# Which attention steps carry the routing arithmetic, and when a new head pair's first values are issued

## The chip, the cores and the metric

The kernel runs on one core of a Trainium2 chip. TensorE (PE in the profile) multiplies matrices, and its weight loads are listed apart as PEld. VectorE is DVE, ScalarE is ACT, GpSimd is POOL, and SyncE (SP) issues transfers. The metric is the device time of one execution in microseconds; the median of several runs counts.

## The reference

The input is 8 items of 256 channels by 32x32 positions, so S=1024 tokens of 256 numbers. Each item goes through a layer of attention over its tokens, a second layer of attention with a norm, and a mixture of experts. Layer 0, which the change concerns, has 8 heads of 64 and takes its softmax over the queries (`axis=1`):

```python
xt = x.reshape(B, C, S).transpose(0, 2, 1)
qkv = (xt @ w_qkv + b_qkv).reshape(B, S, N_HEADS, 3 * D_K)
q, k, v = jnp.split(qkv, 3, axis=-1)
attn = jnp.einsum('bihd,bjhd->bijh', q, k) * SCALE
attn = jax.nn.softmax(attn, axis=1)
res = jnp.einsum('bijh,bjhd->bihd', attn, v).reshape(B, S, N_HEADS * D_K)
res = res @ w_out + b_out + xt
```

The mixture sends every token to the best two of 8 experts:

```python
probs = jax.nn.softmax(logits, axis=-1)
rw, re = jax.lax.top_k(probs, TOP_K)
```

The two weights are divided by their sum, and each chosen expert (matrix, gelu, matrix) adds its weighted result to the token.

## The kernel before

All arithmetic is float32. The loop over items runs layer 0 of item b (`layer0`), then its second attention and norm. The routing of item b is a Python generator, `dispatch`, which is handed to `layer0` of item b+1 and advanced from within it. Experts for items 0 to 6 come after the last layer 0; item 7 is done densely. So layer 0 of item 0 carries no routing, that of items 1 to 7 does.

**Layer 0.** The 8 heads are handled as 4 pairs g, and each pair has 8 blocks j of 128 keys. That is 32 steps, `steps[at]`, and a tail of `LAG` = 2. A score tile has 128 keys on the partitions and 1024 queries. For each step and head h:

- `score(at, h, n)` multiplies keys and queries for one half n of the queries into a two-bank PSUM tile (`psc`). Every matmul uses a 64x64 quarter of the array; four of them, called a set here, run at once in the four quarters. A set is eight records in the profile.
- `first_max` (L410) and `soften` find the maximum of the two halves on VectorE (L410 and L422). ScalarE then takes the exponential and its sum (L432).
- `divide` puts the softmax's divisor into the values (L441, L443).
- `gather_values(at, turn)`, two steps later, multiplies exponentials and values into two one-bank tiles, `po[0]` and `po[1]` (L463). In turn 0 the upper key half goes to one tile and the lower to the other; in turn 1 they change places. Before a row half of the array writes a tile that the other half has just written, a relay (L473) must have seen that one end: a nop on GpSimd for item 0, on SP for the others.

So TensorE's queue for a step is: scores of (at, head 0, half 0) with those of (at−1, head 1, half 1); values of at−2, turn 0; scores of (at, head 0, half 1) with those of (at, head 1, half 0); values of at−2, turn 1.

**PSUM.** Three two-bank buffers (`big`) serve score tiles, projections (`pqk`), the routing's counts (`pcn`) and transposes in turn. Two one-bank buffers (`acc`) hold `po`. When a pair's last values are gathered, ScalarE copies both `po` to `res` (L482); the next pair's first values are written to the same two buffers.

**Projections.** Queries and keys of the next pair are made by `project` in steps j=3 and j=5 of the first three pairs, hence steps 3, 5, 11, 13, 19 and 21. Each has four full-array matmuls (L300, eight records) and two evictions on VectorE (L290).

**Routing.** `gates` makes a softmax over 8 logits for each token and finds the best and second best (about twenty VectorE operations on 128x64, L656 to L725). `dispatch` counts, with two small matmuls into `pcn` (L743, L744), how many tokens before each one go to the same expert. It works out a target row for each token, casts it to an integer (L795) and writes the token there with an indirect transfer on GpSimd (L797): 16 scatters for an item, each with its cast. Before the change the generator is advanced once in step 0 and once in each step from 2 on. Its slice is issued after the step's values of turn 1 and after `first_max(at, 1)`, so it stands on VectorE between the two maxima of (at, head 1). In steps with a projection it is issued after the projection.

A tile framework orders each engine's instructions as they are issued, except where `tc.issue_after` holds one back, and finds the semaphore waits. `tc.add_manual_dep(..., BEHIND)` adds a wait.

Of the kernel before, what the change touches and what calls it, by code (L numbers as in the profile page):

```python
# [11 lines left out]
I32 = mybir.dt.int32  # L12
# [7 lines left out]
def kernel(  # L20
# [349 lines left out]
    def layer0(b, xT, begun, routing):  # L370
# [8 lines left out]
        res = one.tile([P, NPAIR, S], F32, tag="res", name=f"res_{b}")  # L379
        steps = [(g, j) for g in range(NPAIR) for j in range(NT)]  # L380
        LAG = 2
        seconds, turned = {}, {}

        relay = nc.gpsimd if b == 0 else nc.sync
# [98 lines left out]
            return mm  # L483

        last = len(steps) - 1
        for at in range(last + LAG + 1):
            if at <= last:
                score(at, 0, 0)
            if 0 < at <= last + 1:
                score(at - 1, 1, 1)  # L490
                soften(at - 1, 1)
            if at >= LAG:
                gather_values(at - LAG, 0)
            if at <= last:

                with tc.issue_after(seconds[1].ins) if 1 in seconds else nullcontext():
                    first_max(at, 0)
                score(at, 0, 1)
                score(at, 1, 0)
                soften(at, 0)  # L500
                with tc.issue_after(seconds[0].ins):
                    ahead = divide(at - 1) if at > 0 else seconds[0]
                with tc.issue_after(ahead.ins):
                    first_max(at, 1)
            elif at == last + 1:
                divide(last)
            if at == 0:
                begun.rest()
                next(routing, None)
            if at >= LAG:  # L510
                array = gather_values(at - LAG, 1)
            if at <= last:
                g, j = steps[at]
                if g + 1 < NPAIR and j in (3, 5):
                    if j == 3:
                        qks.append([])
                    qks[g + 1].append(project(b, xT, g + 1, len(qks[g + 1])))
                if array is not None:
                    with tc.issue_after(firsts[at, 1].ins), tc.issue_after(array.ins):
                        next(routing, None)  # L520
        for _ in routing:
            pass

# [117 lines left out]
    def gates(b, lT):  # L641


        def tmp(tag):
            return small.tile([P, NT, E], F32, tag=tag, name=f"{tag}_{b}", bufs=1)

        def col(tag):
            return small.tile([P, NT], F32, tag=tag, name=f"{tag}_{b}", bufs=1)

        n = S // NG  # L650
        pt = acc(f"plT_{b}")
        for j in range(n // P):
            nc.tensor.transpose(pt[:, ts(j, P)], lT[:, ts(j, P)], ident)

        l = tmp("g_l")
        nc.vector.tensor_copy(  # L656
            l.rearrange("p (g j) e -> p j g e", g=NG),
            pt[:, :n].rearrange("p (j g e) -> p j g e", g=NG, e=GC)[:, :, :, :E],
        )
        yield  # L660
        m = col("g_m")
        nc.vector.tensor_reduce(m, l, AX.X, ALU.max)
        p = tmp("g_p")
        nc.vector.tensor_sub(p, l, bcast(m, E))
        nc.scalar.activation(p, p, AF.Exp)
        yield
        z = col("g_z")
        nc.vector.tensor_reduce(z, p, AX.X, ALU.add)
        nc.vector.reciprocal(z, z)
        nc.vector.tensor_mul(p, p, bcast(z, E))  # L670
        yield

        def first_of_max(src, tag):
            top, best = col(f"{tag}_top"), col(f"{tag}_best")
            hot = tmp(f"{tag}_hot")
            nc.vector.tensor_reduce(top, src, AX.X, ALU.max)
            nc.vector.tensor_tensor(hot, src, bcast(top, E), ALU.is_equal)
            yield
            nc.vector.tensor_mul(hot, hot, rank)
            nc.vector.tensor_reduce(best, hot, AX.X, ALU.max)  # L680
            nc.vector.tensor_tensor(hot, hot, bcast(best, E), ALU.is_equal)
            return top, hot

        top1, hot1 = yield from first_of_max(p, "g_1")
        yield
        rest = tmp("g_rest")
        nc.vector.scalar_tensor_tensor(rest, hot1, -2.0, p, ALU.mult, ALU.add)
        top2, hot2 = yield from first_of_max(rest, "g_2")
        yield
        total = col("g_total")  # L690
        nc.vector.tensor_add(total, top1, top2)
        nc.vector.tensor_scalar_max(total, total, 1e-12)
        nc.vector.reciprocal(total, total)
        gate = keep.tile([P, 2, NT], F32, tag="gate", name=f"gate_{b}")
        nc.vector.tensor_mul(gate[:, 0], top1, total)
        nc.vector.tensor_mul(gate[:, 1], top2, total)
        return gate, (hot1, hot2)
# [30 lines left out]
    def dispatch(b, n2, l, group):  # L728

        gate, hots = yield from gates(b, l)  # L730
        yield

        def tmp(tag):
            return small.tile([P, NT, E], F32, tag=tag, name=f"{tag}_{b}", bufs=1)


        both = tmp("d_both")
        nc.vector.tensor_add(both, hots[0], hots[1])
        yield
        yield  # L740
        pcn = big(f"pcn_{b}")
        flat = both.rearrange("p i e -> p (i e)")
        nc.tensor.matmul(pcn[:, : NT * E], before, flat, start=True, stop=True)  # L743
        nc.tensor.matmul(pcn[:, NT * E : 2 * NT * E], ones, flat, start=True, stop=True)  # L744
        cn = small.tile([P, 2, NT, E], F32, tag="d_cn", name=f"d_cn_{b}", bufs=1)
        nc.vector.tensor_copy(cn.rearrange("p t i e -> p (t i e)"), pcn[:, : 2 * NT * E])
        yield
        per = small.tile([P, E, NT], F32, tag="d_per", name=f"d_per_{b}", bufs=1)
        nc.vector.tensor_copy(per, cn[:, 1].rearrange("p i e -> p e i"))
        upto = small.tile([P, E, NT], F32, tag="d_upto", name=f"d_upto_{b}", bufs=1)  # L750
        nc.vector.tensor_tensor_scan(
            upto.rearrange("p e i -> p (e i)"),
            later.rearrange("p e i -> p (e i)"),
            per.rearrange("p e i -> p (e i)"),
            0.0,
            ALU.mult,
            ALU.add,
        )
        yield
        rows = tmp("d_rows")  # L760
        nc.vector.tensor_sub(rows.rearrange("p i e -> p e i"), upto, per)
        nc.vector.tensor_add(rows, rows, cn[:, 0])
        counts = keep.tile([P, E], F32, tag="counts", name=f"counts_{b}")
        if group.counts is None:
            nc.vector.tensor_copy(counts, upto[:, :, NT - 1])
        else:
            nc.vector.tensor_add(
                rows, rows, group.counts.unsqueeze(1).to_broadcast([P, NT, E])
            )
            nc.vector.tensor_add(counts, group.counts, upto[:, :, NT - 1])  # L770
        group.counts = counts

        kept = []
        tos = []
        for k in range(2):
            yield
            hot = hots[k]
            sel = tmp("d_sel")
            nc.vector.tensor_mul(sel, hot, rows)
            row = keep.tile([P, NT], F32, tag=f"row{k}", name=f"row{k}_{b}")  # L780
            nc.vector.tensor_reduce(row, sel, AX.X, ALU.add)
            nc.vector.tensor_mul(sel, hot, e_iota.unsqueeze(1).to_broadcast([P, NT, E]))
            exp = keep.tile([P, NT], F32, tag=f"exp{k}", name=f"exp{k}_{b}")
            nc.vector.tensor_reduce(exp, sel, AX.X, ALU.add)
            yield
            to = small.tile([P, NT], F32, tag="d_to", name=f"d_to_{b}_{k}", bufs=2)
            nc.vector.scalar_tensor_tensor(to, exp, float(group.cap), row, ALU.mult, ALU.add)
            kept.append((row, exp))
            tos.append(to)
            group.kept[b] = gate, kept  # L790

        for k in range(2):
            for i in range(NT):
                at = small.tile([P, 1], I32, tag="d_at", name=f"d_at_{b}_{i}_{k}", bufs=4)
                nc.vector.tensor_copy(at, tos[k][:, i : i + 1])  # L795
                view = group.views[2 * (NT * group.items.index(b) + i) + k]
                nc.gpsimd.indirect_dma_start(  # L797
                    out=view[:, :],
                    out_offset=bass.IndirectOffsetOnAxis(ap=at, axis=0),
                    in_=n2[:, i, :],  # L800
                    in_offset=None,
                )
                yield

    def plan(group):

# [371 lines left out]
    begun = Begin(0, next_x)  # L1178
    begun.all()
    prepare()  # L1180
    routing = iter(())
    for b in range(B):
        xT = next_x
        if b + 1 < B:
# [65 lines left out]
```

## Time and profile before

| what | us |
| --- | --- |
| median of 3 runs | 2530.41 (2528.81 to 2532.02) |
| the profiled execution | 2521.92 |
| its span, first to last instruction | 2520.2 |
| TensorE busy | 2421.3 |
| VectorE busy | 1565.1 |
| ScalarE busy | 887.7 |
| GpSimd busy | 386.4 |
| layer-0 scores, L395 on TensorE | 613.4 |
| layer-0 values, L463 on TensorE | 612.8 |

A line of a group names the source line, engine and operation, output and inputs, count, busy time and mean duration in ns, and then the engine's idle time just before these instructions with what ended most of it. A line of the table of waits gives the engine and line that waited, for whom, the total in us, the number of times and the longest. A line of the timeline gives start, duration, engine, line and count, and in brackets the idle time before it with what ended it. TensorE counts as busy while any quarter of it works.

### The profile page before, as it was taken

Reading aid. Unit: us, or ns where it says so; the run is one execution under the profiler, and the core shown is the slowest. Engines: PE = TensorE matmul, PEld = TensorE weight load, DVE = VectorE, ACT = ScalarE, POOL = GpSimd, SP = SyncE. Lnnn points to the kernel's source line nnn. Section 1 sums busy time; section 2 is a strip of 40 time slices with the busy share of each in tenths; the row PEclk is TensorE's granted clock in tenths of the full one; section 3 lists DMA queues with packets and bytes.
Section 4 is the critical chain, followed back from the end, with each engine's and each line's share of the span. In section 5 each row is a group of like instructions: output and inputs, shape, how many; then the busy total and the mean of one; then the engine's idle time right before and its main releaser. Section 6 shows DMA issues by size and latency. Waiting matters only on the chain.

```text
span 2520.2 us, 37152 instructions
## 1 busy us (share of the span) xinstructions
PE 2421.3 (96%) x14015; PEld 1334.8 (53%) x14015; DVE 1565.1 (62%) x3836; ACT 887.7 (35%) x1491; POOL 386.4 (15%) x383
## 2 busy tenths in 40 slices
PE   9999999999999999999999999999999999997799
PEld 3356434653465346533663356335633688875466
DVE  5774677468755884578557855875578643334443
ACT  2541355125512561246225521552154422211222
POOL 0000002000200020002000100010001344434452
PEclk9999999999999999999999999999999999998899
DMA  7992001000100000000000000000001266653353
GB/s 281 385 361 69 34 3 44 6 17 1 35 17 17 1 30 21 17 1 28 24 17 1 25 27 17 1 22 14 1 18 49 91 214 213 217 186 101 98 162 119
DMA packets 82556, 188.23 MB, mean 75 GB/s; under 512 B 13992, under 2 KB 23880, under 8 KB 80584
## 3 DMA queue, kind: packets, MB, share of 16 engines
q1 hardware_dynamic: 57368, 118.65, 13.1%
q0 software_dynamic: 25008, 67.20, 8.6%
q8 instruction: 111, 1.82, 0.3%
q14 instruction: 69, 0.57, 0.1%
HBM read 100.49 MB, written 110.90 MB: 84 GB/s over the span
## 4 chain that ended last, share of the span: by engine, by line
PE 72%; DVE 9%; ACT 3%; issue 2%; DMA 1%; another core or an unknown queue 1%; ACTq 0%; DVEq 0%; SPq 0%; POOLq 0%
PE po L463 13%; PE psc L395 12%; PE pqk L300 8%; PE py L602 7%; PE ps L576 6%; PE pr L542 4%; PE ph L937 4%; PE pe L962 3%; PE pv L336 3%; DVE scrap L422 3%; PE pdy L1144 2%; PE pdh L1120 2%; PE px L561 2%; PE pa L595 2%; ACT ex L432 2%
## 5 line engine op out<-in xcount | busy, mean ns | idle before, releaser
L432 ACT ACTIVATE ex<-psc,nmax 128x1024 f32<-128x1024 f32 x512 | 571.1, 1115 | 528.2 <-DVE scrap L422 408.9
L463 PE MATMUL po<-ex,vs 64*64 64x512 f32 x4096 | 612.8, 593 | 25.4 <-ACT res L482 21.3
L395 PE MATMUL psc<-qk,qk 64*64 64x512 f32 x4096 | 613.4, 596 | 17.3 <-ACT ex L432 16.3
L422 DVE TENSOR_SCALAR_CACHE_REDUCE scrap<-psc,nmax 128x512 f32<-128x512 f32 x512 | 383.9, 750 | 118.3 <-PE psc L395 98.7
L410 DVE TENSOR_REDUCE nmax<-psc 128x1 f32<-128x512 f32 x512 | 350.5, 684 | 11.9 <-PE psc L395 11.9
L395 PEld LDWEIGHTS psc<-qk,qk 64*64 64x64 f32 x4096 | 188.0, 132 | 320.7 <-issue 167.8
L463 PEld LDWEIGHTS po<-ex,vs 64*64 64x64 f32 x4096 | 187.2, 132 | 285.0 <-issue 91.3
L602 PE MATMUL py<-n,aT 128*128 128x256 f32 x1024 | 243.5, 392 | 19.3 <-DVE aT L597 14.5
L797 POOL DMA_INDIRECT rows<-n,d_at x112 | 109.3, 976 | 926.1 <-DVE d_at L795 919.7
L602 PEld LDWEIGHTS py<-n,aT 128*128 128x128 f32 x1024 | 195.4, 195 | 84.2 <-DVE aT L597 52.3
L576 PE MATMUL ps<-nT,xa 128*128 128x512 f32 x512 | 236.5, 592 | 0.0
L300 PE MATMUL pqk<-xT,wqkv 128*128 128x512 f32 x512 | 235.0, 602 | 0.1
L587 ACT ACTIVATE ex<-ps,nmax 128x1024 f32<-128x1024 f32 x64 | 71.3, 1115 | 353.7 <-DVE nmax L584 338.5
L607 DVE SCALAR_TENSOR_TENSOR t<-py,rs,t 128x256 f32<-128x256 f32 x64 | 31.0, 484 | 234.3 <-PE py L602 202.3
L723 POOL TENSOR_TENSOR t<-t,n 128x2048 f32<-128x2048 f32 x8 | 36.3, 4533 | 901.6 <-issue 631.3
L300 PEld LDWEIGHTS pqk<-xT,wqkv 128*128 128x128 f32 x512 | 93.3, 190 | 133.0 <-issue 92.8
L576 PEld LDWEIGHTS ps<-nT,xa 128*128 128x128 f32 x512 | 93.6, 190 | 79.9 <-issue 73.6
L1009 POOL DMA_INDIRECT yk<-y,yat x112 | 112.6, 1006 | 122.4 <-DVE o L1041 71.5
L290 DVE TENSOR_SCALAR qk<-pqk,b_qk 128x512 f32<-128x512 f32 x100 | 75.1, 751 | 85.1 <-PE pqk L300 85.1
L336 PE MATMUL pv<-wqkv,xT 128*128 128x512 f32 x256 | 119.6, 597 | 0.8 <-ACT wqkv L106 0.8
L584 DVE TENSOR_REDUCE nmax<-ps 128x1 f32<-128x1024 f32 x64 | 78.3, 1223 | 59.1 <-PE ps L576 58.6
L542 PE MATMUL pr<-wo,res 128*128 128x256 f32 x512 | 111.8, 379 | 0.0
(191 smaller groups left out, 2441.4 us busy)
## 6 DMA issues: line engine op xcount, KB each, us to landing
rows<-wb SPq DMA_DIRECT2D x7, 8192.0 KB
y<-yb SPq DMA_DIRECT2D x63, 256.0 KB
xT<-in_x_dram SPq DMA_DIRECT2D x7, 1024.0 KB
sums<-t SPq DMA_DIRECT2D x7, 1024.0 KB
o<-sums SPq DMA_DIRECT2D x7, 1024.0 KB
out_dram<-oT SPq DMA_DIRECT2D x14, 512.0 KB
wpack<-in_L_ffn_w_dram SPq DMA_DIRECT2D x4, 1024.0 KB
wb<-in_L_ffn_w_dram SPq DMA_DIRECT2D x16, 256.0 KB
```

The lines of the kernel that those rows point to most:

```text
L300: mm = nc.tensor.matmul(pq[:, ts(n, 512)], wqkv[:, cc, t, ts(g, P)], xT[:, cc, ts(n, 512)], start=(cc == 0), stop=(cc == NCC - 1),)
L336: nc.tensor.matmul(pv, self.xT[:, cc, ts(i, P)], wqkv[:, cc, 2, :], start=(cc == 0), stop=(cc == NCC - 1),)
L395: mm = nc.tensor.matmul(pss[at, h][ts(c, DK), ts(n, 512)], k[r, j * P + c * DK : j * P + (c + 1) * DK], q[r, ts(n, 512)], start=True, stop ...
L410: firsts[at, h] = nc.vector.tensor_reduce(nmax, pss[at, h][:, ts(0, 512)], AX.X, ALU.max, negate=True)
L422: seconds[h] = nc.vector.tensor_scalar(scrap, ps[:, ts(1, 512)], -1.0, nmaxes.pop((at, h)), ALU.mult, ALU.min, accum_out=nmax,)
L432: nc.scalar.activation(ex, ps, AF.Exp, bias=nmax, scale=1.0, accum_out=sums[at][:, h : h + 1])
L463: mm = nc.tensor.matmul(po[n][ts(h, DK), :], vss[at][keys, h, :], exps[at, h][keys, ts(n, 512)], start=(j == 0 and turn == 0), stop=(j == ...
L542: nc.tensor.matmul(pr[:, :C], res[:, g, ts(i, P)], wo[:, g, :], start=(g == 0), stop=(g == NPAIR - 1))
L576: nc.tensor.matmul(psc[:, ts(n, 512)], xa[:, ec, ts(i, P)], nT[:, ec, ts(n, 512)], start=(ec == 0), stop=(ec == NCC - 1),)
L602: nc.tensor.matmul(py[:, :D], aT[:, ts(m, P)], n1[:, m, :], start=(m == 0), stop=(m == NT - 1))
L797: nc.gpsimd.indirect_dma_start(out=view[:, :], out_offset=bass.IndirectOffsetOnAxis(ap=at, axis=0), in_=n2[:, i, :], in_offset=None,)
L1009: nc.gpsimd.indirect_dma_start(out=yk[:, i, k, :], out_offset=None, in_=self.group.y[:, :], in_offset=bass.IndirectOffsetOnAxis(ap=ats[k][ ...
```

## The change

Routing is advanced in step 0 and in the steps of a projection only: steps 3, 5, 11 and 13 hold all of its arithmetic, and it is now issued before the projection. Most `yield`s go; five slices are left: from the logits to the exponential's argument (step 0), softmax and best expert (3), second best and gates (5), counts and row numbers (11), target rows (13). The sixteen casts of 128x1 become two of 128x8. The scatters come one a step from step 14 to 29, each with an added wait for that step's `first_max(at, 1)`.

In the steps 10, 18 and 26, where a new pair's first values are gathered, turn 0 of these values is issued after the step's second score set, directly ahead of turn 1.

```diff
+        PROJECT = [(0, 3), (0, 5)]
+        PROJECT += [(g, j) for g in range(1, NPAIR - 1) for j in (3, 5)]
+        FIRST_SCATTER = PROJECT[3]
...
+        def share(behind=None):
+            try:
+                routing.send(behind)
+            except StopIteration:
+                pass
+
         for at in range(last + LAG + 1):
+            g, j = steps[min(at, last)]
+            late = at > LAG and steps[at - LAG][1] == 0 and (g, j - 1) not in PROJECT
...
-            if at >= LAG:
+            if at >= LAG and not late:
                 gather_values(at - LAG, 0)
...
             if at == 0:
                 begun.rest()
-                next(routing, None)
+                share()
+            if late:
+                gather_values(at - LAG, 0)
             if at >= LAG:
                 array = gather_values(at - LAG, 1)
-            if at <= last:
-                g, j = steps[at]
-                if g + 1 < NPAIR and j in (3, 5):
-                    if j == 3:
-                        qks.append([])
-                    qks[g + 1].append(project(b, xT, g + 1, len(qks[g + 1])))
-                if array is not None:
-                    with tc.issue_after(firsts[at, 1].ins), tc.issue_after(array.ins):
-                        next(routing, None)
+            project_now = at <= last and (g, j) in PROJECT
+            if at <= last and (project_now or (g, j) > FIRST_SCATTER):
+                with tc.issue_after(firsts[at, 1].ins), tc.issue_after(array.ins):
+                    share(firsts[at, 1])
+            if project_now:
+                if len(qks) == g + 1:
+                    qks.append([])
+                qks[g + 1].append(project(b, xT, g + 1, len(qks[g + 1])))
...
         for k in range(2):
...
+            at = small.tile([P, NT], I32, tag=f"d_at{k}", name=f"d_at{k}_{b}", bufs=1)
+            nc.vector.tensor_copy(at, to)
+            ats.append(at)
+        group.kept[b] = gate, kept
 
         for k in range(2):
             for i in range(NT):
-                at = small.tile([P, 1], I32, tag="d_at", name=f"d_at_{b}_{i}_{k}", bufs=4)
-                nc.vector.tensor_copy(at, tos[k][:, i : i + 1])
+                behind = yield
...
-                nc.gpsimd.indirect_dma_start(
+                scatter = nc.gpsimd.indirect_dma_start(
...
-                    out_offset=bass.IndirectOffsetOnAxis(ap=at, axis=0),
+                    out_offset=bass.IndirectOffsetOnAxis(ap=ats[k][:, i : i + 1], axis=0),
...
-                yield
+                if behind is not None:
+                    tc.add_manual_dep(scatter.ins, behind.ins.name, BEHIND)
```

More of the change, by code (lines that the diff above doesn't have):

```diff
@@ L670, in gates @@
         nc.vector.tensor_mul(p, p, bcast(z, E))
-        yield
         def first_of_max(src, tag):
@@ L677, in first_of_max @@
             nc.vector.tensor_tensor(hot, src, bcast(top, E), ALU.is_equal)
-            yield
             nc.vector.tensor_mul(hot, hot, rank)
@@ L682, in first_of_max @@
             return top, hot
-        top1, hot1 = yield from first_of_max(p, "g_1")
-        yield
+        top1, hot1 = first_of_max(p, "g_1")
         rest = tmp("g_rest")
         nc.vector.scalar_tensor_tensor(rest, hot1, -2.0, p, ALU.mult, ALU.add)
-        top2, hot2 = yield from first_of_max(rest, "g_2")
         yield
+        top2, hot2 = first_of_max(rest, "g_2")
         total = col("g_total")
@@ L730, in dispatch @@
         gate, hots = yield from gates(b, l)
-        yield
         def tmp(tag):
@@ L738, in dispatch @@
         nc.vector.tensor_add(both, hots[0], hots[1])
-        yield
         yield
@@ L746, in dispatch @@
         nc.vector.tensor_copy(cn.rearrange("p t i e -> p (t i e)"), pcn[:, : 2 * NT * E])
-        yield
         per = small.tile([P, E, NT], F32, tag="d_per", name=f"d_per_{b}", bufs=1)
@@ L758, in dispatch @@
         )
-        yield
         rows = tmp("d_rows")
@@ L773, in dispatch @@
         kept = []
-        tos = []
+        ats = []
+        yield
         for k in range(2):
-            yield
             hot = hots[k]
@@ L784, in dispatch @@
             nc.vector.tensor_reduce(exp, sel, AX.X, ALU.add)
-            yield
             to = small.tile([P, NT], F32, tag="d_to", name=f"d_to_{b}_{k}", bufs=2)
@@ L788, in dispatch @@
             kept.append((row, exp))
-            tos.append(to)
-            group.kept[b] = gate, kept
+            at = small.tile([P, NT], I32, tag=f"d_at{k}", name=f"d_at{k}_{b}", bufs=1)
+            nc.vector.tensor_copy(at, to)
+            ats.append(at)
+        group.kept[b] = gate, kept
         for k in range(2):
             for i in range(NT):
-                at = small.tile([P, 1], I32, tag="d_at", name=f"d_at_{b}_{i}_{k}", bufs=4)
-                nc.vector.tensor_copy(at, tos[k][:, i : i + 1])
+                behind = yield
                 view = group.views[2 * (NT * group.items.index(b) + i) + k]
-                nc.gpsimd.indirect_dma_start(
+                scatter = nc.gpsimd.indirect_dma_start(
                     out=view[:, :],
-                    out_offset=bass.IndirectOffsetOnAxis(ap=at, axis=0),
+                    out_offset=bass.IndirectOffsetOnAxis(ap=ats[k][:, i : i + 1], axis=0),
                     in_=n2[:, i, :],
@@ L802, in dispatch @@
                 )
-                yield
+                if behind is not None:
+                    tc.add_manual_dep(scatter.ins, behind.ins.name, BEHIND)
     def plan(group):
@@ L1180 @@
     prepare()
-    routing = iter(())
+    routing = (nothing(_) for _ in ())
     for b in range(B):
```

## The prediction, made before the changed kernel ran

> **What bounds the kernel.** I read the page's head first, then its costliest groups.
>
> ```profile
> span 2520.2 us, 37152 instructions
> PE 2421.3 (96%) x14015; PEld 1334.8 (53%) x14015; DVE 1565.1 (62%) x3836; ACT 887.7 (35%) x1491; POOL 386.4 (15%) x383
> ...
> L463 PE MATMUL po<-ex,vs 64*64 64x512 f32 x4096 | 612.8, 593 | 25.4 <-ACT res L482 21.3
> L395 PE MATMUL psc<-qk,qk 64*64 64x512 f32 x4096 | 613.4, 596 | 17.3 <-ACT ex L432 16.3
> ```
>
> TensorE is busy for 96% of the span; everything else has slack on average. So an edit is worth only the TensorE idle it removes, or time in which only half of the array works. The two layer-0 groups show 43 us of counted idle before them. The table of waits names the releasers:
>
> ```profile
> PE po L463 <- ACT res L482: 21.3, 24, 0.9
> PE psc L395 <- ACT ex L432: 16.3, 39, 2.3
> ```
>
> 24 is 8 items by 3 borders between head pairs, 0.89 us each: the first values of a new pair wait until ScalarE has copied the old pair's sums out of PSUM. That is what the second half of the change addresses. What routing costs must be found by comparison, because half-array gaps are not counted as idle. Item 0 routes nothing. Cutting the trace into one stage per item, from the first step's scores to the last's (columns: busy time and count of PE, PEld, DVE, ACT, POOL; clock; DMA), gives items 2, 3 and 0:
>
> ```profile
> 544.50:684.80 140.30, 135.75 (x1030) 53.78 (x1030) 112.87 (x315) 77.67 (x130) 13.20 (x14) 1.00 0.05 19
> 801.10:941.40 140.30, 135.74 (x1030) 53.75 (x1030) 112.88 (x315) 77.66 (x130) 13.16 (x14) 1.00 0.05 19
> 28.60:165.00 136.40, 133.27 (x1024) 52.17 (x1024) 105.82 (x262) 76.12 (x128) 0.00 (x0) 1.00 1.03 382
> ```
>
> Routing adds 3.9 us to layer 0 of an item. Taking the starts of the first row maximum (L410) of successive steps, I split this: step 0 +0.41, steps 2 to 5 +0.07, 6 to 9 +1.25, 10 to 13 +0.95, 14 to 17 +1.26, later nothing. An undisturbed step takes 3.43 us.
>
> The mechanism, VectorE in item 3, and TensorE's weight load after it:
>
> ```profile
> 834.78 0.21 DVE L687 SCALAR_TENSOR_TENSOR g_rest<-g_hot,g_p 128x64 f32<-128x64 f32 x1
> 835.02 0.22 DVE L676 TENSOR_REDUCE g_top<-g_rest 128x8 f32<-128x64 f32 x1
> 835.28 0.23 DVE L677 TENSOR_TENSOR g_hot<-g_rest,g_top 128x64 f32<-128x64 f32 x1
> 835.42 0.74 DVE L422 TENSOR_SCALAR_CACHE_REDUCE scrap<-psc,nmax 128x512 f32<-128x512 f32 x1
> ...
> 837.52 0.21 PEld L395 LDWEIGHTS psc<-qk,qk 64*64 64x64 f32 x8 [1.05 <-ACT ex L432]
> ```
>
> Three small operations stand between the two maxima of a step, so the second maximum is 0.65 us late, its exponential too, and the next scores wait for that score buffer (1.05 us before the load, about 0.5 in a quiet step).
>
> [...] The trace has 214 to 232, so I use about 0.25 us start to start for dependent routing operations. [...] at a border the waiting G holds back the scores queued behind it, although those need nothing of it. [...] a relay of a nop on another engine stands between the two turns; it stays. [...]
>
> **The routing part.** It takes VectorE work out of the steps without projection and puts it into the steps with one (3, 5, 11, 13) and step 0. Removed: the excess of steps 2–5, 6–9 and 14–17, 0.07+1.25+1.26 = 2.58 us per item; 98 of 112 casts go too (143 ns each).
>
> What is added in a projection step must hide. The projection's eight records occupy TensorE 3.43 us, and VectorE's extra work there is two evictions of 0.75 us. Step (0,3) gets 9 operations (2.2 us), (0,5) 11 (some independent, about 1.6), (1,3) the counts' 6–7, (1,5) 12 (about 2.3). Starting 1.04 us after the projection does, the longest bunch puts the second eviction's end at about 4.77 us and the second maximum at 4.79 us from its own scores: it just hides. I charge 0.05 us per item; without cover, (0,3) and (1,5) would cost up to their full 4.5. At step 0 VectorE idles 0.45 us after the copy of the logits, against 0.49 for the two operations moved in: nothing to 0.04; the 0.41 of that step stays.
>
> Of the 16 scatters, each stays one GpSimd instruction (0.97 us), now one a step from step 14 to 29, behind that step's first maximum. GpSimd is 15% busy, its scatters waited 919.7 us on casts, and in items 1 to 7 the relay is on SP. They end before the experts' gather needs them: I charge zero. Late scatters would cost only if the last item's moved past its 1981.3 fetch.
>
> One thing gets worse. The two count matmuls `pcn` now stand before the projection of step 11. Before, in item 2:
>
> ```profile
> 597.25 3.70 PE L300 MATMUL pqk<-xT,wqkv 128*128 128x512 f32 x8
> 600.79 0.33 PE L743 MATMUL pcn<-d_both,before 128*128 128x64 f32 x2
> 600.96 0.39 PE L744 MATMUL pcn<-d_both,ones 128*128 128x64 f32 x2
> 601.27 1.18 PE L395 MATMUL psc<-qk,qk 64*64 64x512 f32 x5
> ```
>
> There the third score buffer went to pqk, and the next scores waited for pqk's second eviction: 0.93 us over item 0. After, pcn takes the buffer free first and the projection itself must wait for the exponential of step 11, which ends 1.42 us after the step's scores began; 1.16 to 1.40 us. Loss 0.23 to 0.47; I take 0.47.
>
> Sum: 2.58 − 0.47 − 0.05 ≈ 2.05, times 7 items = 14.4 us. Bounds: 10 if the bunches in (0,3) and (1,5) together delay a maximum by 0.6, 18 if pcn costs no more than before.
>
> **The border part.** Border of item 0, TensorE and then ScalarE:
>
> ```profile
> 71.06 1.04 PE L395 MATMUL psc<-qk,qk 64*64 64x512 f32 x8
> 73.01 1.13 PE L463 MATMUL po<-ex,vs 64*64 64x512 f32 x6 [0.91 <-ACT res L482]
> 73.92 0.60 PE L395 MATMUL psc<-qk,qk 64*64 64x512 f32 x2
> ```
> ```profile
> 71.27 1.11 ACT L432 ACTIVATE ex<-psc,nmax 128x1024 f32<-128x1024 f32 x1 [0.34 <-DVE rs L441]
> 72.38 1.06 ACT L482 COPY res<-po 128x512 f32<-128x512 f32 x2
> ```
>
> The exponential must end (72.38) before two copies run; the first gives its buffer at 73.0, the second at 73.49. Row halves then run 0.49 us apart until the next full-array matmul. A border costs 1.46 us over 3.43 in its own step, and 0.15 more at the next projection: 1.61 for two borders of an item, 1.46 for the third.
>
> After, the two score sets come first. S(10,0,1) runs 71.92–72.53; S(10,1,0) needs the buffer of that same exponential, so 72.53–73.39. The values still start at 73.01 in one row half and 73.49 in the other, each half as it comes free. Turn 1 follows at once, without a score set between, and so sees the relay openly. The trace has this case once, at the end of layer 0 of the last item:
>
> ```profile
> 1979.13 2.32 PE L463 MATMUL po<-ex,vs 64*64 64x512 f32 x16 [0.33 <-issue]
> ```
>
> Turn to turn is 1.23 there, not 0.86: 0.37 us for matmul end, nop, restart. So turn 1 starts at about 74.40 and 74.70 and the next step's scores at about 75.6 in both halves (before 75.63 and 76.12). Gain 0.5 where the skew used to be paid at the next projection, about 0.4 at the third border: 8 × (0.5+0.5+0.4) = 11.2. Bounds: 1 (0.04 each, if the halves stay skewed) and 21.3 (the whole counted wait).
>
> Total: −14.4 − 11.2 ≈ −25.6. The profiled execution was 2521.9 us for a span of 2520.2, and would be 2496.3. The median of the runs is 8.5 above the profiled one: 2530.4 − 25.6 ≈ **2505 us**.
>
> **Rivals.**
> *Border gain nil.* The chain exponential, copy, copy, values, relay, values has the same length whatever stands in the wait; if the next scores or their exponential hang on it, only 1 of 11.2 comes: −15.4, 2515. For it: both copies and the relay stay. Against: 1.7 us of score work moves into a wait.
> *Border wait gone.* If the relay is covered by the other row half, −21.3 − 14.4: 2495. For it: halves run independently. Against: 1979.13.
> *Bunches don't hide.* If eviction or maximum is pushed in four steps, the routing gain goes and −11.2 is left: 2519; the whole change breaks even at 25.6/7 = 3.7 us per item, near the 4.5 without cover. For it: only 0.02 us of slack in (1,5).
> *Slower: the open relay.* A nop on SP stands behind SP's fetches and stores. A score set hid its delay; back to back nothing does. Above 0.37 + 0.47 + 14.4/24 ≈ 1.44 us of relay at each of 24 borders the change loses; at 2.0 it gives −14.4 + 24 × (1.63 − 0.47) = +13.4: 2544. For it: TensorE's loads waited 42.9 us on SP, 128 times. Against: the longest was 1.0.
> *No effect.* It cannot be void: the built instruction order differs at exactly 24 borders and 7 pcn places on TensorE.
>
> **Chances and range.** Likeliest 0.46 (own range 2499 to 2511), border gain nil 0.19, wait gone 0.17, bunches 0.11, open relay 0.07. The unknowns' bounds give −11 to −39, 2491 to 2519; I take 2492 to 2520, leaving out the relay's case and the tail of the bunches. 0.2%, 5 us, is about what a measurement of this kernel can tell from no change. Faster 0.90 (a quarter of the bunches' case not), same 0.03, slower 0.07.
>
> **What would show it.** Layer 0 of items 2 to 6 at about 136.9 us (138.2 less 1.4 at borders), item 0 at 135.0; steps 6–9 and 14–17 as in item 0; step 11 about 0.4 longer; the wait of po on res below 10 us or gone, with SP in its place, about 0.4 each; border steps 4.4 instead of 4.89. Wrong if projection steps grow over 7.1, or if border steps keep 4.9.

## The result, and the profile after

| | before, us | after, us |
| --- | --- | --- |
| median of 4 runs each | 2530.69 (2528.81 to 2532.02) | 2503.53 (2499.54 to 2504.45) |
| the profiled execution | 2521.92 | 2504.45 |
| layer 0, sum over the 8 items | 1130.4 | 1103.4 |
| layer 0 of item 0 (no routing) | 136.34 | 134.95 |
| layer 0 of items 2 to 6, mean | 140.31 | 136.88 |
| layer 0 of item 7 | 145.90 | 141.04 |
| from there to the end | 546.5 | 556.3 |

The ratio is 0.989 with a 95% interval of 0.9873 to 0.9907: 27.2 us less between the medians, against 25.6 forecast. "Layer 0" is, here and below, the time from the first step's first row maximum to the last step's, read from the trace. The head of the page after, and the two groups of layer 0:

```profile
span 2502.8 us, 37112 instructions
PE 2420.1 (97%) x14015; PEld 1324.5 (53%) x14015; DVE 1565.8 (63%) x3738; ACT 887.6 (35%) x1491; POOL 389.0 (16%) x383
...
L399 PE MATMUL psc<-qk,qk 64*64 64x512 f32 x4096 | 585.9, 594 | 7.3 <-ACT ex L436 7.2
L467 PE MATMUL po<-ex,vs 64*64 64x512 f32 x4096 | 578.9, 593 | 5.6 <-DVE vs L447 4.1
```

The groups' busy times fell by 28 and 34 us, although the matmuls are the same in number and, to 2 ns, in their mean duration, and TensorE's busy time as a whole is the same. The likely reading is that a group counts as busy while any quarter works for it: where one row half runs behind the other, scores and values run at the same time and both are counted. The counted idle before the two groups fell from 43 to 13 us. What TensorE, its weight loads on the last line, wait for now:

```profile
PE psc L399 <- ACT ex L436: 7.2, 11, 2.6
PE pqk L300 <- ACT ex L436: 4.9, 7, 0.7
PEld po L467 <- SPq L477: 60.2, 166, 1.4
```

The wait of the values for ScalarE's copies (21.3 us, 24 times) is gone. Two things came in its place, both named in the prediction: the projection of step 11 waits 0.7 us in each of 7 items for an exponential, and the relay on SP is waited for more often (166 times, 128 before). The stages of item 0, item 2 and item 3 in the table of stretches (columns as before):

```profile
28.30:163.30 135.00, 134.59 (x1024) 51.45 (x1024) 106.11 (x262) 76.13 (x128) 0.00 (x0) 1.00 1.02 382
539.20:676.00 136.80, 135.62 (x1030) 52.63 (x1030) 113.13 (x303) 77.67 (x130) 15.56 (x16) 1.00 0.06 23
792.30:929.30 137.00, 135.73 (x1030) 52.65 (x1030) 113.09 (x303) 77.67 (x130) 15.55 (x16) 1.00 0.06 22
```

VectorE's busy time per item is the same as before to 0.3 us (112.9 to 113.1). It was not made less; it was moved.

**A border.** Item 0, TensorE:

```profile
70.81 2.12 PE L399 MATMUL psc<-qk,qk 64*64 64x512 f32 x14
72.76 0.64 PE L467 MATMUL po<-ex,vs 64*64 64x512 f32 x1
...
73.24 2.28 PE L467 MATMUL po<-ex,vs 64*64 64x512 f32 x14
75.01 1.36 PE L399 MATMUL psc<-qk,qk 64*64 64x512 f32 x8
```

Four sets (32 records) again, but 14 score records now stand ahead of the first values, in the time in which the copies run; before there were 8. The values start 1.95 us after the step (before: 73.01 − 71.06 = 1.95), the other row half 0.48 later, also as before. Turn 1 follows at 74.16 to 74.45. The next step's first score set starts at 75.01 in one row half and by 75.36 in the other, 4.55 after the border began; before, the later half started at 76.12, 5.06 after.

**A routing bunch.** Step 13 of item 2 on VectorE, the fullest of them: the last operations, both evictions, and the second maximum:

```profile
605.27 0.17 DVE L793 SCALAR_TENSOR_TENSOR d_to<-exp,row 128x8 f32<-128x8 f32 x1
605.47 0.17 DVE L796 CAST d_at<-d_to 128x8 int32<-128x8 f32 x1
605.55 1.40 DVE L290 TENSOR_SCALAR qk<-pqk,b_qk 128x512 f32<-128x512 f32 x2
607.01 0.75 DVE L426 TENSOR_SCALAR_CACHE_REDUCE scrap<-psc,nmax 128x512 f32<-128x512 f32 x1
```

The bunch runs from 603.15 to 605.64, the evictions back to back behind it, and the second maximum starts with no idle time ahead of it. TensorE finishes the scores of that maximum at 606.95, just when the evictions end, so it is not late: the step takes 7.09 us, as the same step does in item 0. Elsewhere there is some room: in step 3, 0.28 us of idle are left before that maximum.

**The counts.** Step 11 of item 2, TensorE:

```profile
590.20 0.43 PE L752 MATMUL pcn<-d_both,before 128*128 128x64 f32 x2
590.47 0.39 PE L753 MATMUL pcn<-d_both,ones 128*128 128x64 f32 x2
591.57 3.70 PE L300 MATMUL pqk<-xT,wqkv 128*128 128x512 f32 x8 [0.71 <-ACT ex L436]
```

The counts took the free score buffer and the projection waits for the exponential of that step (ScalarE, 590.31 to 591.42). So the 1.37 us from the first count matmul to the projection are about half the count matmuls' own time on TensorE and half a wait.

### The profile page after: what moved, and what is told of

Its sections match the earlier page's. It is cut to its first block, busy times and chain, and to the rows that moved or that the text cites. A ratio compares the mean times of both kernels' runs of the same rounds, so it can differ in the third digit from the quotient of the medians.

```text
span 2502.8 us, 37112 instructions
## 1 busy us (share of the span) xinstructions
PE 2420.1 (97%) x14015; PEld 1324.5 (53%) x14015; DVE 1565.8 (63%) x3738; ACT 887.6 (35%) x1491; POOL 389.0 (16%) x383
## 4 chain that ended last, share of the span: by engine, by line
PE 76%; DVE 4%; another core or an unknown queue 2%; ACT 2%; issue 2%; DMA 1%; ACTq 0%; DVEq 0%; SPq 0%; POOLq 0%
PE po L467 15%; PE psc L399 15%; PE pqk L300 8%; PE py L617 8%; PE ps L591 6%; PE ph L945 4%; PE pr L557 4%; PE pe L970 4%; PE pv L336 3%; PE px L576 2%; PE pdy L1152 2%; PE pa L610 2%; PE pdh L1128 1%; ACT ex L436 1%
## 5 line engine op out<-in xcount | busy, mean ns | idle before, releaser
L399 PE MATMUL psc<-qk,qk 64*64 64x512 f32 x4096 | 585.9, 594 | 7.3 <-ACT ex L436 7.2
L467 PE MATMUL po<-ex,vs 64*64 64x512 f32 x4096 | 578.9, 593 | 5.6 <-DVE vs L447 4.1
L399 PEld LDWEIGHTS psc<-qk,qk 64*64 64x64 f32 x4096 | 181.5, 132 | 304.4 <-issue 161.1
L467 PEld LDWEIGHTS po<-ex,vs 64*64 64x64 f32 x4096 | 174.5, 132 | 284.0 <-issue 96.8
```

Of the source, the lines that this page charges most:

```text
L399: mm = nc.tensor.matmul(pss[at, h][ts(c, DK), ts(n, 512)], k[r, j * P + c * DK : j * P + (c + 1) * DK], q[r, ts(n, 512)], start=True, stop ...
L467: mm = nc.tensor.matmul(po[n][ts(h, DK), :], vss[at][keys, h, :], exps[at, h][keys, ts(n, 512)], start=(j == 0 and turn == 0), stop=(j == ...
```

## The experiments

The runs were spread over chips on which the kernel before took 2492 to 2531 us. On two of them it was profiled: its layer 0 is the same to 0.2 us in sum, and the difference lies behind layer 0 of item 7, in the tail (546.5 us against 516.5). TensorE's half-clock windows (below) add up to 46.7 us of the one tail and 23.3 of the other. At the 0.50 of the clock that they show this explains at most 12 of the 30 us; the larger part is TensorE's idle time, 49.7 us against 29.3, and what causes it is open. So ratios are to the kernel before on the same chip, and layer-0 times are compared across all.

**The kernel before, once more.** No edit.

> The kernel before, once more. In the profile of before, 546.5 us pass from the last step of item 7's layer 0 to the end; in that of after 556.4, with one stall of 13 us in the dense part. Theory A (the stall belongs to the execution and not to the change): the median stands within 0.2% of before, its layer-0 stages repeat within 0.1 us each (140.3 for items 2 to 6), and what this profile differs by from the first one of before (2521.9) lies after layer 0 of item 7. Theory B (the change causes the stall): the tail is again within 1 us of 546.5 and the profiled execution within 2 us of 2522.

Measured: ratio 1.0003 (0.9996 to 1.001). Layer 0 sums to 1130.6, items 2 to 6 at 140.32. Behind item 7's layer 0 it takes 516.5 us instead of 546.5, on another chip. The layer-0 stages of items 0 to 6 repeat to 0.02 us, that of item 7 to 0.17 (0.1 was expected): they can be compared across chips, and the tail can't. This speaks for theory A only in so far as the tail varies by itself; the stall is settled two runs below.

**The border part alone.** In the kernel before:

```diff
+            late = LAG < at <= last and steps[at - LAG][1] == 0
...
-            if at >= LAG:
+            if at >= LAG and not late:
                 gather_values(at - LAG, 0)
...
+            if late:
+                gather_values(at - LAG, 0)
```

> The border part alone, on the kernel before. Theory A (the two parts add up): item 0, which has no routing, shows 134.95 as in after; items 2 to 6 go from 140.3 to 138.9; the border steps from 4.89 to 4.39; in all 8 x 1.39 = 11 us, ratio 0.9956, about 2519.5. Rival (routing slices, which here still stand in the border steps 10 and 18, delay the exponential that the moved scores wait for): items 2 to 6 gain less than 0.9, in all under 8 us.

Measured: ratio 0.9961 (0.9947 to 0.9975), 11.8 us between the medians. Item 0 134.94, items 2 to 6 138.88, border steps 4.38 to 4.40. The gain is 1.39 to 1.44 us per item, also where routing stands in border steps. Theory A holds. Layer 0 in sum is 12.9 shorter, not 11.4, because item 7 lost 1.4 more; see the half clock below.

**The routing part alone.** In the changed kernel:

```diff
-            late = at > LAG and steps[at - LAG][1] == 0 and (g, j - 1) not in PROJECT
+            late = False
```

> The routing part alone: after without the moved first values. Theory A: items 2 to 6 at 138.2 (140.3 less 2.1), border steps at 4.89, step 11 at 8.6, item 7 gains 1.3 more than the others; in all 7 x 2.1 + 1.3 = 16 us, ratio 0.9937, about 2514.5. Rival (most of the gain needs both parts, since the routing stood in border steps too): under 12 us.

Measured: ratio 0.9943 (0.9926 to 0.9959), 15.1 us between the medians, 15.5 in layer 0. Items 2 to 6 at 138.09, 2.22 less than before. Step 11 takes 8.38, not 8.6. And item 7 gained no more than the others (1.97): here theory A was wrong. The two parts nearly add: 1.44 + 2.22 = 3.66 against 3.43 with both. The missing 0.23 is step 11, 8.58 with both. When the border ends earlier, the projection still waits, for the same exponential: its wait in TensorE's table is 0.7 us each time with both (4.9 in 7) and 0.5 here (3.4 in 7).

**The counts behind the projection.**

```diff
-            if at <= last and (project_now or (g, j) > FIRST_SCATTER):
+            counts_now = (g, j) == (1, 3)
+            if at <= last and not counts_now and (project_now or (g, j) > FIRST_SCATTER):
...
                 qks[g + 1].append(project(b, xT, g + 1, len(qks[g + 1])))
+                if counts_now:
+                    with tc.issue_after(firsts[at, 1].ins), tc.issue_after(array.ins):
+                        share(firsts[at, 1])
```

> After, but the slice with the two count matmuls is issued behind the projection of step 11 and not ahead of it. Theory A (the projection then gets its score buffer first and the counts wait, as before the change): step 11 back from 8.58 to 8.14, 0.44 for each of 7 items, 3.1 us below after, about 2500.4. Rival (the counts' VectorE work, now behind both evictions, makes the second maximum of that step late instead): step 11 or 12 grows by as much, no difference to after.

Measured: ratio 0.9896 (0.9879 to 0.9912), which can't be told from the 0.989 of after. Layer 0 of items 2 to 6 is 136.55, 0.33 less than in after: steps 11 and 12 take 8.44 and 3.37 instead of 8.58 and 3.57. Three quarters of the expected 0.44 are there, and the waits of pqk on the exponential are out of TensorE's table. That the order of these two costs about 0.3 us per item is shown; in the time of the whole kernel it doesn't show.

**The changed kernel, once more.** No edit.

> The changed kernel once more, beside the next three. Theory A (what the first profile of it lost after layer 0 belongs to that execution): layer 0 repeats (136.9 for items 2 to 6, 134.95 for item 0), ratio near 0.989 again, and the stall of 13 us in the dense part is not there. Rival (the stall comes with the change): it is there again, with a stage after layer 0 that is some 10 us longer than that of before.

Measured: ratio 0.9892 (0.9874 to 0.9909). Items 2 to 6 at 136.88, item 0 at 134.95, and in TensorE's waits nothing of the 13 us that the first profile of after had:

```profile
PE pdy L1152 <- ACT dh L1137: 13.1, 1, 13.1
```

So that stall, in the dense experts of item 7, belongs to one execution. VectorE stood idle for 20.45 us ahead of it and the profile shows no releaser on this core; what held it is open. Shorter idle times of this kind, 5.9 to 13.7 us at the longest, stand before the same statement in eight other profiles, the first one of before among them (7.5 us), so the change did not bring them. The stall is long enough to explain why the two first profiled executions differ by only 17.5 us where the medians differ by 27.2.

**Turn 0 inside the second score set.** What the expectation below calls the two score sets are two calls of `score`, the two halves of one set of four matmuls: head 0's, on one row half of the array, and head 1's, on the other, which is also the row half that waits for the second copy. Turn 0 now stands between them. In the changed kernel:

```diff
                 score(at, 0, 1)
+                if late:
+                    gather_values(at - LAG, 0)
                 score(at, 1, 0)
...
-            if late:
-                gather_values(at - LAG, 0)
```

> The changed kernel, with turn 0 of a new pair's first values between the two score sets of the border step and not behind both. Theory A (the gain of the border is the second score set, which fills the copies' wait, and the relay then costs little): the row half that waits for the second copy is a score set later, border and the next step together cost 0.4 to 0.5 more than in after, so item 0 goes from 134.95 back to about 136.1 and the sum of all borders loses 8 to 11 us. Rival (the open relay between the two turns takes most of what the moved sets bring, so covering it again is worth as much): item 0 at 135.0 or less.

Measured: ratio 0.994 (0.9922 to 0.9959). Item 0 takes 136.34 and items 2 to 6 138.09, to 0.01 us what they take with no border part at all. Yet the wait that the border part was aimed at is gone from TensorE's table:

```profile
PE po L467 <- ACT res L486: 0.3, 1, 0.3
```

It was 22.0 us in the kernel with routing alone. Nothing was won with it, because the idle time now lies in one row half at a time, where the table doesn't count it. In item 0 the first score set ends at 71.93. Head 0's matmuls keep one row half busy until 72.78, and its values follow at 72.84; the values of the other half start at 73.32, so that half stands still for 1.4 us. In after it runs head 1's scores in this time (72.28 to 73.36). The whole gain of a border thus comes from head 1's half of the second set. Theory A holds: item 0 loses a little more than it said (136.34, not 136.1), and layer 0 in sum some 10 us.

**One of two copies on VectorE.**

```diff
-                for n in range(NH2):
-                    nc.scalar.copy(res[:, g, ts(n, 512)], po[n])
+                nc.scalar.copy(res[:, g, ts(0, 512)], po[0])
+                nc.vector.tensor_copy(res[:, g, ts(1, 512)], po[1])
```

> The changed kernel, with one of the two copies of a finished pair on VectorE and the other on ScalarE, so that both buffers are free 0.5 us earlier. Theory A (what is left of a border, 4.38 against 3.43, is the chain exponential, two copies, values, relay): 0.3 to 0.4 less at each of 24 borders, 7 to 10 us below after. Rival (VectorE has no room there: its copy stands ahead of a second maximum and delays the exponential behind it): border steps unchanged or longer, no gain.

Measured: ratio 0.9888 (0.9871 to 0.9905). Border steps fall from 4.38–4.40 to 3.90, but the step ahead of each grows from 3.43 to 3.82: 0.1 us per border is left of 0.5, 0.32 per item without routing, where 0.9 to 1.2 was expected. The rival was nearer in its reason: VectorE, with its copy of 0.68 us ahead of a maximum, has little room there.

**The same slices, one step later.** In the changed kernel:

```diff
-        FIRST_SCATTER = PROJECT[3]
+        SHARES = [(0, 4), (0, 6), (1, 4), (1, 6)]
+        FIRST_SCATTER = SHARES[3]
...
-            if at <= last and (project_now or (g, j) > FIRST_SCATTER):
+            if at <= last and ((g, j) in SHARES or (g, j) > FIRST_SCATTER):
```

> The changed kernel, with the same four slices of routing each one step later: in steps 4, 6, 12 and 14, which have no projection. Theory A (it is the projection's 3.4 us on TensorE that hides them): each bunch now delays a second maximum and the scores behind it by its length less some 0.4 us, together about 6 us for each of 7 items; layer 0 of items 2 to 6 at 141 to 143, longer than before the change, about 40 us over after. Rival (VectorE has room enough in any step, the gain came from fewer slices and casts): under 138.

Measured: ratio 1.0062 (1.0042 to 1.0083), slower than before the change. Undisturbed items take 142.0 to 142.3, 5.2 over after. Step 4 takes 5.52 instead of 3.57, step 6 4.80, step 12 (counts) 4.96, step 14 5.75. VectorE in step 4 of item 2, and TensorE after it:

```profile
570.30 0.22 DVE L699 SCALAR_TENSOR_TENSOR g_rest<-g_hot,g_p 128x64 f32<-128x64 f32 x1
570.44 0.74 DVE L427 TENSOR_SCALAR_CACHE_REDUCE scrap<-psc,nmax 128x512 f32<-128x512 f32 x1
```
```profile
572.55 2.84 PE L300 MATMUL pqk<-xT,wqkv 128*128 128x512 f32 x6 [1.69 <-ACT ex L437]
```

The nine operations that cost nothing in step 3 start at 568.28 here, hold the second maximum back until 570.44, and TensorE is idle for 1.69 us. The projection is the cover; fewer slices and casts are not what made the gain. The counts cost 1.39 us in step 12 too, where no projection competes:

```profile
606.44 0.43 PE L753 MATMUL pcn<-d_both,before 128*128 128x64 f32 x2
606.71 0.39 PE L754 MATMUL pcn<-d_both,ones 128*128 128x64 f32 x2
607.80 1.09 PE L400 MATMUL psc<-qk,qk 64*64 64x512 f32 x8 [0.70 <-ACT ex L437]
```

Half of it is again the two matmuls' own time, 0.66 us, and half the 0.70 us that the next scores wait for a score buffer. The seven VectorE operations behind the counts could be a third reason; here they end at 609.05, and the second maximum starts at 608.97, when the scores for it have just ended (608.89).

**Three edits together, and one of them alone.** The counts behind the projection and the split copies, both as above, and the plan of the experts' blocks (the last item's `plan_blocks`) in two halves:

```diff
+        parts = plan_blocks(group)
+        with tc.issue_after(evicted[B - 1, NPAIR - 1, 0].ins):
+            next(parts)
         with tc.issue_after(evicted[B - 1, NPAIR - 1, 1].ins):
-            return plan_blocks(group)
+            return next(parts)
...
         nc.vector.tensor_scalar_min(e_of, e_of, float(E - 1))
+        yield
...
-        return row_at, w_at
+        yield row_at, w_at
```

> The changed kernel with three edits that the runs so far point to: the count matmuls behind the projection (0.33 us for each of 7 items), one of a pair's two copies on VectorE (0.32 for each of 8), and the plan of the experts' blocks split in two, the first half behind the first eviction of step 19 and the rest behind the last of step 21 in item 7. Theory A (they add up, and the half-clock window that an idle of 2.4 us can bring in item 7 is gone with that idle): layer 0 some 7 us shorter than in after, 1096 to 1098 in sum, ratio to before 0.986 to 0.987. Rival (the split only moves the plan's stalls into step 19 to 21): item 7 not under 140.5, ratio 0.988.

> The changed kernel with the split plan alone. Theory A: item 7's excess over items 2 to 6 goes from 4.2 us to about 2, no idle of TensorE over 1 us is left in its layer 0, and no window of half clock in it. Rival: the excess stays at 4 or more, in other steps.

> The changed kernel beside the two above, for their comparison on one chip: ratio 0.989 again, layer 0 of items 2 to 6 at 136.9.

Measured: all three 0.9883 (0.9866 to 0.9899), after beside it 0.9892 (0.9875 to 0.9908). Medians 2491.07 and 2493.66, layer 0 in sum 1099.1 and 1103.3. The first two edits give what they gave alone, 0.67 per item. So layer 0 is 4 us shorter, not 7. The split plan, of which there is one execution by itself, gives nothing: item 7 at 141.84 with it alone (141.04 to 141.60 without), since the plan's stalls, in steps 21 and 22 of item 7 in after, only spread over 19 to 24. Rival right. The fastest kernel here is 2.6 us ahead of after by its median, which the intervals don't tell apart.

## Why the prediction was right, and where it was not

**Borders.** Forecast 0.5, 0.5 and 0.4, 1.4 an item and 11.2 in all. Measured 1.39 in item 0 and 1.44 in items 2 to 6, 11.4 in all without item 7's extra. The step's own length (4.4) came out as worked, and so did the start of the next scores in the later row half (75.6; measured 75.36 with the step 0.25 earlier). The other half starts 0.34 us before it, where the forecast had both together. The border-alone run shows the sum; the run with turn 0 inside the second set shows the cause. Both border rivals fall. "Gain nil" said that the chain of exponential, copies, values and relay keeps its length; it doesn't, since the next scores start 0.5 us earlier. "Wait gone" took the counted wait for the gain: it did go, 21.3 us, and 11.4 came of it. The open relay cost what the one example of before gave: the second row half's turns lie 1.20 us apart in item 0 (1.23 in the example). The rival of an open relay falls with it. No run leaves the relay out; whether the values need it was not shown.

**Routing.** Forecast 2.58 removed, 0.47 lost at the counts, 0.05 lost at the bunches: 2.05 an item. Measured with both parts: steps 2 to 5 now cost 0.06 over item 0, steps 6 to 9 and 14 to 17 nothing (in three items 0.16 to 0.3 once), step 11 1.36 over item 0 against 0.90: 0.46 lost. Together this is 2.04 of the 3.43: the excess of items 2 to 6 over item 0 went from 3.97 to 1.93. With routing alone it is 2.22, since there the counts lose 0.23, the lower end. The bunches hide, the fullest with no slack left (0.02 was forecast), and 5.2 us per item come back without the projection. The rival that they do not hide falls, but by little: in step 13 evictions and scores end together, so one more small operation could be expected to show. No run tried it.

**What was not forecast.** By these two terms layer 0 should shorten by 25.6 us, and it did so by 27.0. The difference is item 7, 1.4 us more than the others. The routing and border sums do not contain it; it is no merit of the change that can be relied on (next section but one). The agreement of the medians, 27.2, with 25.6 is thus good to about 1.5 us, and in part luck. The rest of the execution was rightly taken to be untouched: on the one chip where kernels with and without the parts were profiled side by side, the tail took 516.5 us before, 516.8 with the border part and 517.9 with the routing part.

**The step that was loose.** "Removes the excess" took 2.58 as gone in whole and this held; but the two parts were summed as if independent. The experiments show 0.23 us per item of overlap at step 11. It was hidden in the sum by taking the upper end, 0.47, for the counts: right for both parts together, 0.24 too much for routing alone. The prediction gives no reason for the upper end, so this fit is luck.

**Readings that were off.** Two numbers of the prediction don't follow from the trace of before. The second maximum of the step shown in item 3 is 0.44 us later than in the same step of item 0 (it starts 1.24 us after the first maximum there, against 0.80), not 0.65; 0.43 is also what that step costs over item 0. The sum doesn't use this number. And in step 11 of item 2 the exponential ends at 598.24, 0.99 us after the projection begins and no scores start 1.42 us before that. The range for the counts, 0.23 to 0.47, holds all the same: 0.23 with routing alone and 0.46 with both parts. The prediction's 214 to 232 are ns for an operation of the routing on 128x64; in the trace of before the elementwise ones of `gates` took 212 to 228 ns. Its 0.25 us from start to start holds: in item 3 the three shown start 0.24 and 0.26 us apart.

## What to carry to other kernels

An engine that is off the bound (VectorE here, busy for 63% of the span) still has room only at certain places: find the step in which the bounding engine is busy with something that doesn't need the other, and put all the small work there; the same operations one step later made the kernel slower than it was (ratio 1.0062). Where a wait is unavoidable, move into it the work that is free of it in queue order, and judge by the stage's length, not by the wait's count: idle time in part of an array, 1.4 us of it at the border with turn 0 inside the second set, was in none of the tables used here. Small work that takes one more of a few rotating buffers costs more than its own time: the counts took 1.4 us in step 11 and in step 12, and half of it was a wait for a buffer.

## What the runs showed of the hardware

The clock granted to TensorE was 0.50 instead of 1.00 in some stretches, the half-clock windows here and above; those shown in layer 0 last 3.4 us each. With routing alone, stretches of 6.4 and 3.4 us in item 7, around the plan's stall, and then the stretch of 3.4 us behind it in after (the clock is the third column from the end):

```profile
1923.10:1929.50 6.40, 3.45 (x32) 1.13 (x36) 6.31 (x23) 2.80 (x5) 3.30 (x4) 1.00 0.20 61
1929.50:1932.90 3.40, 3.40 (x24) 1.20 (x20) 1.88 (x4) 2.01 (x4) 1.96 (x2) 0.50 0.89 262
```
```profile
1919.40:1922.80 3.40, 3.40 (x32) 1.28 (x36) 2.98 (x9) 2.41 (x4) 2.25 (x3) 1.00 0.86 282
```

The stall is the same (2.55 us of idle), but one run then has half the clock and does 24 records where the other does 32. The window stands in item 7 of both profiles of before, of routing alone and of the split copies; their item 7 exceeds items 2 to 6 by 5.6 to 6.2 us. In after's three profiles, in the border part alone, with the counts behind the projection, with turn 0 inside the second set and in both runs with the split plan it is absent, and the excess is 4.1 to 5.0. That is the unforecast 1.4 us.

With the slices one step later, items 1 to 7 each have the same idle of TensorE, 1.92 to 1.93 us, behind step 14, but only items 1, 3, 5 and 7 show a window of half clock there, at 364.3, 883.1, 1402.0 and 1920.8 us; items 3 and 5 took 143.71 instead of the 142.0 to 142.3 of the others. (Item 7 has a second window behind the plan's stall.) Here are two stretches of 3.41 us around this idle, in item 3 with a window directly behind it, and in item 4 with none:

```profile
879.72:883.13 3.41, 1.49 (x16) 0.34 (x12) 3.15 (x12) 1.70 (x3) 0.00 (x0) 1.00 0.00 0
1139.13:1142.54 3.41, 1.50 (x16) 0.31 (x8) 3.15 (x12) 1.21 (x2) 0.00 (x0) 1.00 0.00 0
```

TensorE was busy for 1.49 us in the one and for 1.50 in the other, so the length of the idle doesn't tell by itself whether a window follows.

The stall in item 7 shows the same. It is 2.35 us long both in before and in the border part alone. In before a window follows: the clock is 1.00 from 1941.00 to 1944.41, where TensorE is busy for 1.35 us, and 0.50 from there to 1947.82. In the border part alone the stall ends at 1933.40, and the clock is 1.00 from 1927 to 1942. So an idle of 2 us cost more in one item or kernel than in another, and what decides it was not shown. Both profiles of before have the window and none of after's three has it; whether this holds for every execution of a kernel was not tried.
